# Seven block products instead of eight for gate and up, with a reordered pair pipeline

## Chip, cores and metric

The kernel runs on one core of one Trainium2 chip. The metric is device time in microseconds for one execution. Three executions of the kernel before took 2089.64, 2089.70 and 2092.26 us; the median is 2089.7.

## What is computed

For 32 sequences of 512 tokens with 256 channels, all in float32: a normalized copy of x goes through a delta-rule attention block and an MLP, is added to x, and then a gated MLP is added. Cut to what matters:

```
h = layernorm(normalize(x));  q, k, v = split(h @ gates_w + gates_b);  lr = h @ lr_w + lr_b
k = k / norm(k);  A = tril(k k^T, -1) + I;  u = solve_triangular(A, v)
y = (q k^T) (lr * u);  x1 = normalize(x) + y @ out_w + out_b
x2 = x + x1 + relu(layernorm(x1) @ w1 + b1) @ w2 + b2          # 256 wide
g  = normalize(x2)
out = x2 + (silu(g @ Wg^T) * (g @ Wu^T)) @ Wd^T                # Wg, Wu: 768 x 256, Wd: 256 x 768
```

The weights Wg, Wu and Wd come as integers and are scaled by 1/127. The change is mainly in how the two products of the last line, gate and up, are formed.

## The kernel before, in words

Sequences are worked in 16 pairs (NS = 2). A pair passes through stages, and the stages of three pairs overlap: while gate and up of pair `old` run, the triangular solution of pair `new` is interleaved with them, the pair `following` is loaded and normalized, and the down projection of pair `older` ends. The order of TensorE, VectorE, ScalarE and SP is the order in which the Python code issues instructions (`manual_schedule`); GpSimd's order is left to the framework's scheduler. Work that runs beside the products, a `Side` (L136), is a generator that is advanced in proportion to the columns that TensorE has been given: each product calls `spend(columns)`, and INVERT, PREPARE and INVERT_FIRST say over how many columns a Side is to be spread.

The stages that the prediction uses:

- **Values** (`values_phase`, L1174): gather (pf, L805), through_values (pz), through_keys (pm; its sum m with a bias row is VectorE's, L828), answer (po_d, L844, then statistics L408 to L419), for each sequence of the pair. Before, the keys (pk, L562) and grams (pg, L591) of the following pair stand between these.
- **Inverse** (`invert`, L632): of the following pair's 32x32 diagonal blocks, on VectorE alone. `give` (L601) writes the blocks to DRAM (`given`), SP reads them back spread over partitions (`blocks`), then come a reciprocal (L649), a few sums and fifteen rounds of a product (L683) and a reduction (L689). The result goes through DRAM (`found`, `yb`, `yfull`).
- **Solution** (`solve` and `merge`, L770 and L712): merges the inverted blocks (pw and py, L730 to L763) and solves (pr L784, pu L794), step by step, with VectorE and ScalarE between the steps.
- **Middle** (`middle`, L1055): the residual sum (L903), the MLP (`mlp_in` pa L911, `mlp_out` po_m L844), the normalization for gate and up. `normed` writes h by ScalarE (L422) and transposes 32x32 blocks by VectorE (L460); they go out to DRAM (`way`) and `turned` fetches them back feature-wise (hT).
- **Gate and up** (`gated`, L931): for each of 6 blocks of 128 hidden features and each sequence, two products of 128x512 for gate and two for up (contraction over 256 channels), SiLU by ScalarE from PSUM (L947), product by VectorE from PSUM (L949).
- **Down** (`Down`, L952): already by seven block products instead of eight. `plain` makes three of them (po_x) and then mixes hidden blocks by four GpSimd sums (L987 to L990), `combined` makes the other four (po_y) and adds the parts with VectorE and GpSimd.

A matmul of float32 shows as two records each on PE and PEld. PSUM has three pools: ps_a (3 tiles), ps_f (4 tiles) and one fixed tile.

The inner loop of gate and up reads, with the calls that advance the Sides:

```
for f in range(NF):
    nc.tensor.matmul(pp, lhsT=w[:, f, ts(o, P)], rhs=s.hT[:, f, :],
                     start=(f == 0), stop=(f == NF - 1))
    spend(512)
    if f == NF - 1:
        if name == "gate":
            nc.scalar.activation(natural(g), grouped(pp), AF.Silu)
        else:
            nc.vector.tensor_tensor(natural(g), natural(g), grouped(pp), ALU.mult)
```

Of the kernel before, what the change touches and what calls it, by code (L numbers as in the profile page):

```python
# [22 lines left out]
def kernel(  # L23
# [40 lines left out]
    LEAD = 8  # L64
    NS = 2
    PLAIN = 12
    PREPARE = 12 * 1024
    INVERT = 26 * 1024
# [29 lines left out]
    class Columns:  # L98
# [3 lines left out]
        def __init__(self, n):  # L102
# [4 lines left out]
            first = small.tile([B, self.nc, B], F32, tag="unit", name=f"first{n}", bufs=2)  # L107
# [206 lines left out]
    wgT = const.tile([P, NF, HID], F32, name="wgT")  # L314
    wuT = const.tile([P, NF, HID], F32, name="wuT")
# [6 lines left out]

    class Dequant:
        def __init__(self, src, name, tag, bufs, k):
# [3 lines left out]
            for r0 in range(0, rows // P, k):  # L328
                m = min(k, rows // P - r0)
                wi = wk.tile([P, m, self.cols], I32, tag=tag, name=f"{name}_i{r0}", bufs=bufs)  # L330
                self.parts.append((r0, m, wi))
# [23 lines left out]
    def whole_rows(dst):  # L355
        def put(cc, r0, m, pt):
            nc.scalar.copy(dst[:, cc, r0 * P : (r0 + m) * P], pt)

        return put

    class Combined:


        def __init__(self):
            self.b12 = wk.tile([P, NP, P], F32, tag="p", name="b12")
# [70 lines left out]
    def to_features(src, dst, tag, plain=False):  # L436

        for f in range(NF):
            pt = ps_f.tile([P, 512], F32, tag="mm", name=f"tp_{tag}_{f}")
# [43 lines left out]
    def normalized(s):  # L483
# [15 lines left out]
        yield  # L499

        left = small.tile([P, NT], F32, tag="left", name=f"left_{n}")
        for c in range(NT):
# [4 lines left out]
            yield  # L507
# [9 lines left out]
        for c in range(NT):  # L517
# [4 lines left out]
            nc.gpsimd.tensor_copy(s.hlast[:, c, :], s.a[:, c, C - 1 : C])  # L522
            nc.gpsimd.tensor_copy(s.a[:, c, C - 1 : C], s.r2[:, 1, c : c + 1])
            yield
        if n // NS == 1:
# [14 lines left out]
    def rates(s):  # L540
        n = s.n
        s.lr = small.tile([P, NT], F32, tag="lr", name=f"lr_{n}", bufs=5)
        for c in range(NT):
            junk = wk.tile([P, C], F32, tag="junk", name=f"jl_{n}_{c}", bufs=1)
# [5 lines left out]
        nc.vector.tensor_tensor(s.lr, s.lr, s.r2[:, 0, :], ALU.mult)  # L550
        yield

    def to_keys(s):
        to_features(s.a, s.ag, f"a{s.n}", plain=True)
# [58 lines left out]
    def norms(g, given, seqs):  # L613
# [7 lines left out]
        yield 4  # L621
# [5 lines left out]
        for slot, s in enumerate(seqs):  # L627
            s.kn = kn[:, slot, :]
            nc.vector.tensor_tensor(s.kn, s.kn, s.r2[:, 0, :], ALU.mult)
        yield  # L630

    def invert(g, given, seqs):  # L632
# [20 lines left out]
        )  # L653

# [7 lines left out]
        )  # L662
        nc.vector.tensor_tensor(odd, odd, above, ALU.add)
# [3 lines left out]
        yield 2 * B  # L667
# [12 lines left out]
        for i in range(2, B, 2):  # L680
# [11 lines left out]
            yield 2 * (B + i)  # L692

# [76 lines left out]
    def solve(s):  # L770
# [6 lines left out]
        for i in range(NT):  # L777
# [19 lines left out]
            nc.scalar.mul(s.dp[:, i, :], pu, s.lr[:, i : i + 1])  # L797
            yield

    def contract(s, lhs, rhs, nk, name):  # L800

        s.pp = ps_a.tile([P, NF, C], F32, tag="mm", name=f"p{name}_{s.n}")
# [302 lines left out]
    def first_values(seqs, following, norms_, inverse, given):  # L1105
# [39 lines left out]
        for s in seqs:  # L1145
            fetch_residual(s)
# [214 lines left out]
```

## Time and profile before

| | |
|---|---|
| median of three executions | 2089.7 us |
| the profiled execution | 2090.19 us, span 2088.4 us |
| granted TensorE clock, mean | 0.995 |
| TensorE weight load busy | 1373.5 us (66%) |
| VectorE busy | 1232.8 us (59%) |
| ScalarE busy | 703.9 us (34%) |
| GpSimd busy | 729.9 us (35%) |
| steady pair, start of pf to start of the next pair's pf | 124.2 to 126.3 us |
| first product on TensorE | 21.84 us |

A row of a group names line, engine, operation, the tiles (out<-in) and shapes; after the bar stand busy time, mean nanoseconds of one, and the engine's idle time in front of such instructions with what ended it. A row of the timeline has start, duration (us), engine, line, operation, tiles and count; in brackets stands the idle time before it. A row of windows has the stretch, its length, busy time and instruction count of PE, PEld, VectorE, ScalarE and GpSimd, the granted clock, the DMA share and GB/s.

### The profile page before, as it was taken

To read this page: it belongs to the slowest core of one execution; us is meant where nothing else is said; L and a number is where in the kernel's file an instruction comes from. 1 tells how busy PE (TensorE), PEld (TensorE's weight loads), DVE (VectorE), ACT (ScalarE), POOL (GpSimd) and SP (SyncE) were. 2 spreads that over 40 slices of the span, in tenths; PEclk is the share of its full clock that TensorE was granted. 3 is DMA by queue.
4 is the path that set the end of the run, shared out by engine and by line. 5 is a ranking of instruction groups with operands and counts; after the bars stand their busy time and mean duration, and the time that the engine had idled before them with its cause. 6 is when DMAs were issued, how large, how long until landed. Compare 5 with 4: busy or idle time off the path is not lost.

```text
span 2088.4 us, 27547 instructions
## 1 busy us (share of the span) xinstructions
PE 2028.3 (97%) x9134; PEld 1373.5 (66%) x9134; DVE 1232.8 (59%) x3691; ACT 703.9 (34%) x1788; POOL 729.9 (35%) x1008
## 2 busy tenths in 40 slices
PE   5899999999999999999999999999999999999998
PEld 2565766757576675766767576675766767576675
DVE  3656474755747576474855747476474855747252
ACT  3333423324242343423334242343423334242231
POOL 3411332525224342432525224251422525124244
PEclk9999999999999999999999999999999999999999
DMA  3211332332324223332332324223332432323020
GB/s 90 83 34 28 84 98 62 109 90 56 91 71 127 63 74 89 92 90 62 107 95 54 94 69 128 62 74 89 87 95 62 113 88 54 94 69 107 22 61 21
DMA packets 249605, 163.90 MB, mean 78 GB/s; under 512 B 82129, under 2 KB 225112, under 8 KB 249464
## 3 DMA queue, kind: packets, MB, share of 16 engines
q1 hardware_dynamic: 246272, 160.30, 27.7%
q10 hardware_dynamic: 3112, 1.71, 0.3%
q8 instruction: 73, 1.20, 0.2%
q14 instruction: 68, 0.56, 0.1%
q0 software_dynamic: 80, 0.14, 0.0%
HBM read 96.02 MB, written 66.06 MB: 78 GB/s over the span
## 4 chain that ended last, share of the span: by engine, by line
PE 84%; DVE 7%; DMA 4%; issue 1%; POOL 1%; ACT 1%; SPq 1%; ACTq 0%; POOLq 0%; DVEq 0%
PE pup L940 16%; PE pgate L940 15%; PE pg L591 6%; PE po_d L844 5%; PE pf L805 5%; PE po_y L970 5%; PE pk L562 5%; PE po_x L970 4%; PE pr L784 4%; PE pa L911 4%; PE po_m L844 3%; PE pu L794 3%; PE pm L805 3%; PE pz L805 3%; DMA hT_f<-way_f 1%
## 5 line engine op out<-in xcount | busy, mean ns | idle before, releaser
L940 PE MATMUL pgate<-hT_f,wgT 128*128 128x512 f32 x768 | 366.5, 600 | 8.2 <-DMA hT_f<-way_f 6.3
L940 PE MATMUL pup<-hT_f,wuT 128*128 128x512 f32 x768 | 364.3, 596 | 0.0
L949 DVE TENSOR_TENSOR hid<-hid,pup 128x512 f32<-128x512 f32 x192 | 130.7, 681 | 243.7 <-PE pup L940 240.9
L947 ACT ACTIVATE hid<-pgate 128x512 f32<-128x512 f32 x192 | 113.7, 593 | 404.4 <-PE pgate L940 404.4
L940 PEld LDWEIGHTS pgate<-hT_f,wgT 128*128 128x128 f32 x768 | 142.4, 190 | 153.6 <-issue 135.6
L940 PEld LDWEIGHTS pup<-hT_f,wuT 128*128 128x128 f32 x768 | 143.1, 190 | 146.0 <-issue 139.7
L987 POOL TENSOR_TENSOR hid<-hid 128x384 f32<-128x384 f32 x64 | 63.1, 1007 | 383.0 <-DVE hid L949 383.0
L970 PEld LDWEIGHTS po_y<-wdS,hid 128*128 128x128 f32 x1536 | 176.5, 192 | 8.4 <-issue 6.0
L828 DVE TENSOR_TENSOR m<-pm,obrow 128x256 f32<-128x256 f32 x32 | 13.6, 424 | 280.5 <-ACT m L827 280.4
L970 PE MATMUL po_y<-wdS,hid 128*128 128x128 f32 x1536 | 176.8, 275 | 0.0
L391 POOL TENSOR_TENSOR r_m<-ve_m,neghalf 128x4 f32<-128x4 f32 x32 | 32.4, 1013 | 332.5 <-DVE nmn_m L417 332.4
L591 PE MATMUL pg<-kT 128*128 128x256 f32 (+3 forms) x512 | 144.1, 433 | 0.1
L970 PEld LDWEIGHTS po_x<-wdS,hid 128*128 128x128 f32 x1152 | 132.9, 192 | 8.3 <-issue 4.8
L970 PE MATMUL po_x<-wdS,hid 128*128 128x128 f32 x1152 | 134.1, 275 | 0.0
L591 PEld LDWEIGHTS pg<-kT 128*128 128x128 f32 x512 | 92.0, 190 | 52.9 <-issue 22.4
L562 PE MATMUL pk<-ag,wa 128*128 128x512 f32 x256 | 119.8, 602 | 0.9 <-ACT ag L443 0.9
L911 PE MATMUL pa<-hT_m,w1s 128*128 128x512 f32 x256 | 116.4, 597 | 0.8 <-DMA hT_m<-way_m 0.6
L844 PE MATMUL po_m<-w2s,act 128*128 128x256 f32 x512 | 116.3, 380 | 0.3
L805 PE MATMUL pf<-a,dp 128*128 128x256 f32 x512 | 113.1, 379 | 0.0
L422 ACT ACTIVATE h_f<-a,mr_f,r_f 128x256 f32<-128x256 f32 x112 | 60.6, 594 | 154.0 <-POOL mr_f L419 118.3
L805 PEld LDWEIGHTS pf<-a,dp 128*128 128x128 f32 x512 | 97.3, 190 | 19.6 <-issue 7.2
L689 DVE TENSOR_REDUCE beside<-xt 128x16 f32<-128x64 f32 (+14 forms) x225 | 103.8, 461 | 7.7
(202 smaller groups left out, 3458.0 us busy)
## 6 DMA issues: line engine op xcount, KB each, us to landing
a<-in_L_attn_x_dram SPq DMA_DIRECT2D x32, 512.0 KB, 4.6
x<-in_L_attn_x_dram SPq DMA_DIRECT2D x32, 512.0 KB, 5.5
out_dram<-a SPq DMA_DIRECT2D x64, 256.0 KB, 4.5
way_m<-turn_m SPq DMA_DIRECT2D x120, 128.0 KB, 2.6
hT_m<-way_m SPq DMA_DIRECT2D x30, 512.0 KB, 3.6
way_a<-turn_a SPq DMA_DIRECT2D x112, 128.0 KB, 2.3
ag<-way_a SPq DMA_DIRECT2D x28, 512.0 KB, 3.8
way_f<-turn_f SPq DMA_DIRECT2D x112, 128.0 KB, 2.3
```

Source lines behind the costliest of these rows:

```text
L562: nc.tensor.matmul(pk, lhsT=wa[:, f, ts(o, P)], rhs=s.ag[:, f, :], start=(f == 0), stop=(f == NF - 1),)
L591: nc.tensor.matmul(pg[:, :w], lhsT=s.kT[:, f, ts(j, P)], rhs=s.kT[:, f, j * P :], start=(f == 0), stop=(f == NF - 1),)
L689: nc.vector.tensor_reduce(xc[:, :, i : i + 2], t[:, :, :, :w], axis=AX.X, op=ALU.add)
L784: nc.tensor.matmul(pr, lhsT=s.go[j][:, ts(i - j - 1, P)], rhs=p_[:, j, :], start=(j == 0), stop=(j == i - 1),)
L805: nc.tensor.matmul(s.pp[:, o, :], lhsT=lhs[:, c, ts(o, P)], rhs=rhs[:, c, :], start=(c == 0), stop=(c == nk - 1),)
L844: nc.tensor.matmul(self.po[:, c % 2, :], lhsT=src[:, ts(c, P)], rhs=self.w[:, f, :], start=(f == 0), stop=(f == self.nk - 1),)
L911: nc.tensor.matmul(pa, lhsT=w1s[:, f, ts(o, P)], rhs=s.hT[:, f, :], start=(f == 0), stop=(f == NF - 1),)
L940: nc.tensor.matmul(pp, lhsT=w[:, f, ts(o, P)], rhs=s.hT[:, f, :], start=(f == 0), stop=(f == NF - 1),)
L947: nc.scalar.activation(natural(g), grouped(pp), AF.Silu)
L949: nc.vector.tensor_tensor(natural(g), natural(g), grouped(pp), ALU.mult)
L970: nc.tensor.matmul(po[:, i, :], lhsT=self.A[block][:, j, :], rhs=wdS[:, j, slot, :], start=(j == 0), stop=(j == NP - 1),)
L987: nc.gpsimd.tensor_tensor(A[1, 0], A[1, 0], A[1, 1], ALU.add)
```

## The change

- Gate and up: for two hidden blocks j and the two halves of the channels and of the tokens, seven products of 128x256 take the place of eight. The stationary operands are seven stored blocks (`wgS`, `wuS`, made once by GpSimd sums, `Stationary`); the moving operands are four blocks or sums of blocks of hT (`mixed`, four GpSimd sums a sequence). One PSUM tile `y` gets the products 1, 6, 7 and 4 added one upon another and is copied by ScalarE between them; a second tile `z` gets 2, 5 and, upon 5, 3. Sums and the gate's product are spread over ScalarE, VectorE and GpSimd (`Unit`), with some issued a few steps later (`later`). The steps of a unit are interleaved with those of the unit before.
- Order of a pair: keys, grams and `give` of the following pair move from the values stage into the second half of gate and up (EARLY = 56, every second step). The inverse's Side is begun at the start of the values stage and finished before answer(two). The Down work that stood in the middle moves partly into the values stage. The merge and the first solution step stand between the MLP's products in `middle`; the rest of the solution follows in gate and up, one step in three.
- `normed(two, "m")` and its fetch move into `middle`; `normed` of the second sequence for gate and up is done in steps within gate and up.
- GpSimd's order is now the order of issue, too.
- The residual x is fetched and its bias added separately (`fetch_residual`, `biased`), later and into other buffers. The scaling of dp by lr moves from ScalarE to VectorE; the products of lr and kn with r move from VectorE to GpSimd; the copies of single columns in `normalized` are joined, four in one.
- `contract` and `answer` take PSUM from ps_f. Weight integers are loaded into other buffers; the first pair is reordered accordingly.

The diff, cut to its core:

```diff
-    LEAD = 8
+    LEAD = 16
...
-    PLAIN = 12
-    PREPARE = 12 * 1024
-    INVERT = 26 * 1024
+
+    LOAD, NORM, STORE, TURN, START, MIX, EARLY = 1, 3, 8, 15, 16, 28, 56
+    PREPARE = 13 * 1024
+    INVERT = 17 * 1024
...
+        def put(self, cc, r0, m, pt):
+            dst, some = self.dst, slice(r0 // 2, (r0 + m) // 2)
+            pt = pt.rearrange("p (j i r) -> p j i r", i=2, r=P)
+            nc.scalar.copy(dst[:, some, cc, :], pt[:, :, 0, :])
+            nc.scalar.copy(dst[:, some, 3, :] if cc else self.a21[:, some, :], pt[:, :, 1, :])
+            if cc == NF - 1 and r0 + m == NH:
+                b = lambda i: dst[:, :, i, :]
+                two = lambda o, x, y, op: nc.gpsimd.tensor_tensor(o, x, y, op)
+                two(b(4), self.a21, b(3), ALU.add)
+                two(b(6), b(0), self.a21, ALU.subtract)
+                two(b(5), b(4), b(0), ALU.subtract)
+                two(b(2), b(1), b(5), ALU.subtract)
...
-            nc.scalar.mul(s.dp[:, i, :], pu, s.lr[:, i : i + 1])
+            nc.vector.tensor_scalar(s.dp[:, i, :], pu, s.lr[:, i : i + 1], None, ALU.mult)
...
+        minus(t1, block(0, 1), block(0, 0))
+        yield
+        minus(t2, block(1, 1), t1)
+        yield
+        minus(t3, block(1, 1), block(0, 1))
+        yield
+        minus(t4, block(1, 0), t2)
+        yield
...
+        def copy(self, name, src):
+            t = wk.tile([P, T // 2], F32, tag="x2", name=f"{name}_{self.name}", bufs=4)
+            nc.scalar.copy(t, src)
+            return t
+
+        def p1(self, later):
+            self.y = ps_f.tile([P, 512], F32, tag="mm", name=f"py{self.name}")
+            self.y = self.y[:, : T // 2]
+            self.mul(self.y, 1, True, True)
+            self.top = wk.tile([P, 2, T // 2], F32, tag="fz", name=f"top_{self.name}", bufs=4)
+            nc.scalar.copy(self.top[:, 0], self.y)
+
+        def p2(self, later):
+            self.z = ps_f.tile([P, 2, T // 2], F32, tag="mm", name=f"pz{self.name}")
+            self.mul(self.z[:, 0], 2, True, True)
+
+        def p5(self, later):
+            self.mul(self.z[:, 1], 5, True, True)
+            self.five = self.copy("five", self.z[:, 1])
+
+        def p6(self, later):
+            self.mul(self.y, 6, False, True)
+            nc.scalar.copy(self.top[:, 1], self.y)
+
+        def p7(self, later):
+            self.mul(self.y, 7, False, True)
+            v = self.copy("v", self.y)
+            if self.up:
+                nc.gpsimd.tensor_tensor(v, v, self.five, ALU.add)
+                later(5, lambda: nc.gpsimd.tensor_tensor(
+                    self.out(1, 1), self.out(1, 1), self.half(v), ALU.mult
+                ))
+            else:
+                to = self.out(1, 1)
+                nc.gpsimd.tensor_tensor(to, self.half(v), self.half(self.five), ALU.add)
+                later(10, lambda: nc.scalar.activation(to, to, AF.Silu))
+
+        def p4(self, later):
+            self.mul(self.y, 4, False, True)
+            if self.up:
+                nc.vector.tensor_tensor(
+                    self.out(1, 0), self.out(1, 0), self.half(self.y), ALU.mult
+                )
+            else:
+                nc.scalar.activation(self.out(1, 0), self.half(self.y), AF.Silu)
+
+        def p3(self, later):
+            self.mul(self.z[:, 1], 3, False, True)
...
+            if self.up:
+                nc.vector.tensor_tensor(self.top, self.top, self.z, ALU.add)
+                later(4, lambda: nc.gpsimd.tensor_tensor(
+                    natural(g), natural(g), grouped(flat(self.top)), ALU.mult
+                ))
+            else:
+                nc.vector.tensor_tensor(
+                    natural(g), grouped(flat(self.top)), grouped(flat(self.z)), ALU.add
+                )
+                later(9, lambda: nc.scalar.activation(g, g, AF.Silu))
...
+            steps = [
+                (new, "p1"), (old, "p7"), (old, "p3"), (new, "p6"), (old, "p4"), (new, "p2"),
+                (new, "p5"),
+            ]
...
+        mlp_in(one, 0)
+        normed(two, "m")
+        mlp_in(one, 1)
+        turned(two, "m")
         residual(one)
...
+        if rest:
+            sides_[0].finish()
+        more()
         mlp_out(one, 0)
         mlp_out(one, 1)
+        for d in rest[:2]:
+            d.store()
+        step()
+        more()
+        step()
+        normed(one, "f")
         mlp_in(two, 0)
+        step()
+        residual(two)
         mlp_in(two, 1)
...
+        step()
         mlp_out(two, 0)
...
+        turned(one, "f")
+        if not rest:
+            sides_[1].finish()
+            next(sides_[0].gen)
+            sides_[0].finish()
+        whole(mixed(one))
+        step()
         mlp_out(two, 1)
...
+        sides_ = sides_of(begun(following, given), INVERT)
...
+        some(10)
         whole(gather(one))
-        prep.finish()
+        next(units).both()
+        fetch_residual(one)
+        whole(through_values(one))
         some(2)
+        next(units).both()
+        whole(through_keys(one))
+        third = next(units)
+        third.plain()
+        answer(one)
+        third.mix()
+        biased(one)
         whole(gather(two))
...
+        normed(one, "m")
+        next(combined)()
+        fetch_residual(two)
         whole(through_values(two))
...
+        last = next(units)
+        last.plain()
         whole(through_keys(two))
...
+        turned(one, "m")
         in_order(a)
...
+        biased(two)
+        next(combined)()
+        sides_[1].finish()
+        next(sides_[0].gen)
         answer(two)
+        last.mix()
         in_order(b)
...
+                for i, _ in enumerate(gated(old)):
+                    if i >= EARLY and i % 2 == 0 and solved:
+                        next(early, lambda: None)()
+                    if i % 3 == 2:
+                        solved = next(sol, sol) is sol
```

## The prediction, made before the change was run

> **What bounds the kernel now.** I read the page's busy shares first, then the windows of single pairs, then the order of instructions in time.
>
> ```profile
> PE 2028.3 (97%) x9134; PEld 1373.5 (66%) x9134; DVE 1232.8 (59%) x3691; ACT 703.9 (34%) x1788; POOL 729.9 (35%) x1008
> 463.07:587.31 124.24, 123.96 (x562) 84.13 (x561) 77.65 (x232) 42.75 (x109) 44.52 (x61) 1.00 0.32 86
> L940 PE MATMUL pgate<-hT_f,wgT 128*128 128x512 f32 x768 | 366.5, 600 | 8.2 <-DMA hT_f<-way_f 6.3
> L940 PE MATMUL pup<-hT_f,wuT 128*128 128x512 f32 x768 | 364.3, 596 | 0.0
> ```
>
> TensorE is the bound: 97% of the span, and in a steady pair 123.96 of 124.24 us, at a granted clock of 1.00. A pair leaves VectorE 46 us idle, ScalarE and GpSimd about 80 each. Overlapping records make busy time longer than pace, so I take pace from starts in the timeline:
>
> ```profile
> 741.70 3.62 PE L844 MATMUL po_d<-m,aT 128*128 128x256 f32 x16
> 745.15 4.48 PE L591 MATMUL pg<-kT 128*128 128x512 f32 x16
> 791.33 1.88 PE L940 MATMUL pup<-hT_f,wuT 128*128 128x512 f32 x4
> 793.05 1.88 PE L940 MATMUL pgate<-hT_f,wgT 128*128 128x512 f32 x4
> ```
>
> A float32 matmul is two records ("passes"). Sixteen of 256 columns take 745.15 - 741.70 = 3.45, 0.2155 us each; four of 512 take 1.72, 0.429 each. Passes of 128 columns come out at 0.112. Counted with these (each row's count divided by 16 pairs), a pair needs: gate and up 96 x 0.429 = 41.2, all else 81.6, together 122.8 us. Twelve pairs from 463.07 to 1965.55 average 125.2, so 2.4 us a pair are waits.
>
> **The change, part by part.** *Products.* Two blocks of 128 hidden features were 8 passes of 512 (3.43 us); they become 14 of 256 (3.02). There are 32 x 3 x 2 = 192 such units: 192 x 0.415 = **79.7 us** off TensorE, 5.0 a pair. All passes change weights already in the rows above, so more weight loads cost nothing that the 0.2155 does not hold.
>
> *Sums.* A gate and an up unit (6.03 us of TensorE) now give ScalarE eight copies of 256 (0.37 by the L796 row) and three SiLUs (0.47, 0.47, 0.59): 4.5 us for 1.2 before. VectorE gets 0.68 + 0.68 + 0.42 for 1.36. GpSimd gets three sums of 256 columns and a product of 512. L991 shows 0.74 for 256, L988 1.00 for 384, so 1.33 for 512: 3.55 us. Block sums of the moving side (L975) are 4 x 0.74 = 3.0 a sequence. Six units of each kind and two sequences a pair, with the scaling of dp moved to VectorE (8 x 0.42) and column copies joined: ScalarE 43 to 59, VectorE 78 to 84, GpSimd 44.5 to about 69 us, of a pair of 120. None becomes the bound by its sum. The pieces matter where TensorE waits for them.
>
> The Trainium skill speaks against the move to GpSimd (GPSIMD Engine Reference, "Elementwise — side-by-side cycle accounting": two-input float32 work takes about 2.6 cycles an element there, roughly twice VectorE's time, so VectorE stays the rule). By its figure 256 columns are an estimated 0.56 us, by L991 0.74; the row decides. On VectorE the 27 us of GpSimd would be some 15, but nothing is on TensorE's path while GpSimd keeps within its 6.03 us. The same page's "Specifications" warn that both engines share SBUF interfaces when VectorE reads two SBUF inputs, and here the trace agrees:
>
> ```profile
> 752.75 1.75 DVE L903 TENSOR_TENSOR a<-a,x 128x1024 f32<-128x1024 f32 x1
> 753.37 1.99 POOL L988 TENSOR_TENSOR hid<-hid 128x384 f32<-128x384 f32 x1
> 764.41 1.22 DVE L903 TENSOR_TENSOR a<-a,x 128x1024 f32<-128x1024 f32 x1
> ```
>
> Side by side 1.75 and 1.99; apart 1.22 and 1.00. Most new VectorE work reads PSUM with one input, so I charge only 0.5 us to a residual sum that meets a block sum, off the path.
>
> *The round trip.* One PSUM tile is added to four times, with a ScalarE copy between. A copy starts 0.20 after the next pass would, takes 0.37, and TensorE goes on 0.06 later (m at 117.12 + 0.37, po_d at 117.55): 0.63. Mostly two other products (0.86) lie between: covered, by 0.23. Between p7 and p4 of the last unit there is one: 0.2 a pair.
>
> *Order.* Keys and grams of the next pair go into the second half of gate and up, the inverse from there into the values stage, the merge and first solution steps between the MLP products. What was spread over 26 x 1024 columns (INVERT; at 1.68 ns a column 45 us) gets 17 x 1024, 29 us. Costed by queue, with t = 0 at the first pf:
>
> ```profile
> 749.67 0.27 ACT L595 COPY gd<-pg 128x128 f32<-128x128 f32 x1
> 749.96 1.73 SPq L609 DMA_DIRECT2D given<-gd  x4
> 753.37 0.53 SPq L636 DMA_DIRECT2D blocks<-given  x1
> 758.90 0.36 DVE L649 RECIPROCAL few<-blocks 128x32 f32<-128x32 f32 x1 [4.40 <-DMA blocks<-given]
> 764.01 0.22 DVE L683 TENSOR_TENSOR xt<-beside,blocks 128x64 f32<-128x64 f32 x1
> ```
>
> From issuing the diagonal blocks on SP to the reciprocal: 8.94 us; the inverse's beginning: 5.1. In the new order the last gram ends three products before t = 0, 1.5 with the wait above; so (copy of the gram, 0.2 + 0.27) the blocks go out at -1.0 and VectorE can start at 7.9, after idling. Behind that, in VectorE's one queue, stand before answer(two)'s input: beginning 5.1, fifteen loop rounds 13.2 (summed from the same timeline), two m sums 0.7, answer(one) with statistics 3.5, its transposes 1.5, one combined() 1.3: 25.3, plus 0.7 waiting for po_d. So m(two) is there at 33.9. TensorE would need it after pf 2 x 3.45, pz and pm 4 x 1.72, po_x 4 x 2.02, po_y 2 x 2.7, po_d 3.45 = 30.7. **Wait: 3.2 us a pair**, part at answer(one), part at answer(two).
>
> The middle, followed in the same way: po_d(two) runs from 34.0 to 37.4, VectorE ends its statistics at 39.4, GpSimd's r and mr end at 40.9, ScalarE's four h copies at 43.0. Behind those copies on ScalarE stands the ReLU of mlp_in(one, 1), so po_m starts at 43.9 where TensorE was free at 37.4 + 3.43 + 2.7 = 43.5: 0.4. On VectorE the residual sum, a combined() and both statistics of one end at 49.4, the first merge's three transposes at 50.3, its rhs and the second's transposes at 51.6; TensorE is free at 50.1 and 50.9: pw waits 0.2 and 0.75. The transposes for normed(one, "f") stand behind the merge's copies and end at 55.2; from there to hT_f it takes 7.7 (774.97 to 782.67 before), so 62.9, against 62.3: 0.6. **About 2.0 in all**; the merge's own waits now (PE on xparts, 11.5 us in the run) are replaced, not added. Then r_f(two) stands behind four L975 sums on GpSimd, its h copies stop ScalarE, and behind them wait top_up, v and the next solution step: **0.8**. Bounds for each of these three: nothing if the front work comes 1 us earlier, twice as much if VectorE lags 2 us more; I take what the rows give.
>
> Sum: 3.2 + 2.0 + 0.8 + 0.2 = 6.2 for 2.4 now: 3.8 given back, times 14 pairs = 53 us. The first pair's finish of the inverse leaves over half of 18.3 us to VectorE at once, with 4.7 of TensorE work before a product needs VectorE: +6 (2 to 8). The last unit's sums on GpSimd stand before the last po_x, and own() is queued behind the mixes: +2. -79.7 + 53 + 6 + 2 = -19. The profiled execution took 2090.2 us (span 2088.4), half a microsecond over the median 2089.7: **2071**.
>
> **Rivals.** *The backlog does not reach TensorE.* If the inverse begins 1 us sooner (blocks landed in 4.0 to 6.3 us) and PSUM slots and slack take the rest, the 3.2 fall away: 14 x 3.2 = 45, giving 2026. For it: everything else in that stage has cover. Against: the 25.3 us are queued in order, and 30.7 - 7.9 is only 22.8.
>
> *Slower: foreign ScalarE work breaks the round trip.* Place: gate and up. Twelve operations a pair with no TensorE work of their own (four h of 0.59, eight centering passes of 0.50) enter ScalarE's queue between the copies; the cover to spare is 0.23. If each falls before a copy that is due, it costs 0.5 - 0.23 = 0.27: 3.2 a pair, 49 over 15, less the 11 that I already charge for h: 2109. With a wait for nm or mr in front, twice that. It decides from 19 / 15 = 1.3 us a pair, 0.11 an operation. For it: h_f waited 118.3 us in all for mr_f before. Against: most centering passes now follow p7, where the next copy is two products off.
>
> *No saving at all*, because shorter passes do not run in half the time: excluded by 0.2155 against 0.429.
>
> **How the numbers follow.** Main case, most of the saving given back, 2050 to 2094: 0.45, of it 0.07 within 0.2% (about what a measurement of this kernel can tell from no change, 4 us) and the rest faster. Backlog absorbed, 2010 to 2050: 0.2. Slower, 2094 to 2150: 0.35. So faster 0.58, same 0.07, slower 0.35. Leaving out 0.08 below and 0.12 above, the range is 2030 to 2118.
>
> **What would show it.** Gate and up products of 256 columns at 0.2155, 2688 of them; TensorE waits on VectorE's m before po_d near 3 us a pair, with VectorE without idle from the reciprocal to the end of the inverse; pw on xparts about 1; the reciprocal some 8 us after pf. Wrong would be: no idle time at po_d (first rival), or idle time in front of p6, p4, p3 on ScalarE's copies throughout gate and up (second).

## The result, and the profile after

Four executions took 2150.16 to 2152.22 us, median 2150.5, against 2090.05 for the kernel before beside it (four, 2089.64 to 2092.26): ratio 1.0287, 95% interval 1.0273 to 1.0301. The change is slower by 60 us; the forecast was 2071. The profiled execution has a span of 2148.7 us at a mean granted clock of 0.987.

From the page of the kernel after: busy shares, the chain of work that ended last by engine, and three groups.

```profile
PE 1998.5 (93%) x10286; PEld 1590.2 (74%) x10286; DVE 1372.7 (64%) x3851; ACT 924.0 (43%) x2532; POOL 1112.0 (52%) x1400
...
PE 50%; DVE 24%; DMA 8%; issue 7%; ACT 6%; POOL 3%; SPq 1%; ACTq 0%; DVEq 0%; POOLq 0%
...
L1043 POOL TENSOR_TENSOR v_up<-v_up,five_up 128x256 f32<-128x256 f32 x96 | 69.8, 727 | 241.4 <-ACT v_up L1017 241.4
...
L1003 PE MATMUL pygate<-hS,wgS 128*128 128x256 f32 x576 | 174.8, 385 | 5.2 <-ACT v_gate L1017 2.4
...
L1067 POOL TENSOR_TENSOR hid<-hid,top_up 128x512 f32<-128x512 f32 x96 | 122.4, 1275 | 0.0
```

The same chain in the kernel before:

```profile
PE 84%; DVE 7%; DMA 4%; issue 1%; POOL 1%; ACT 1%; SPq 1%; ACTq 0%; POOLq 0%; DVEq 0%
```

TensorE was the path for 84% of the span and is now for 50%; VectorE's share went from 7% to 24%. Counted from the starts of all passes, each at its own pace (0.2155 us for 256 columns and so on), TensorE's work fell from 1967.8 to 1887.9 us: 79.9 saved, as forecast. What lies beyond that pace between two starts is waiting. It rose by 140 us.

Where, the windows tell. First a steady pair of the kernel after (start of pf to the next), then another cut into its stages: values (to the first po_d of the second sequence that waits), middle (to the first product of gate and up), gate and up. Columns: stretch, length, busy time and count of PE, PEld, VectorE, ScalarE, GpSimd, clock, DMA share, GB/s.

```profile
503.20:632.40 129.20, 121.93 (x633) 96.95 (x632) 86.20 (x243) 56.34 (x157) 67.36 (x86) 1.00 0.30 82
632.47:665.30 32.83, 31.48 (x204) 28.73 (x202) 28.45 (x87) 9.36 (x23) 22.48 (x26) 1.00 0.29 82
665.30:696.04 30.74, 28.07 (x174) 21.06 (x175) 24.94 (x73) 9.52 (x23) 16.06 (x23) 1.00 0.40 112
696.04:760.69 64.65, 62.59 (x256) 47.19 (x257) 33.72 (x85) 37.49 (x112) 28.89 (x38) 1.00 0.24 69
```

A pair of the kernel before in nearly the same cuts:

```profile
714.00:745.15 31.15, 31.15 (x126) 23.34 (x125) 9.39 (x35) 10.83 (x24) 8.15 (x8) 1.00 0.18 55
745.15:782.67 37.52, 37.20 (x233) 30.67 (x232) 30.15 (x96) 14.68 (x37) 24.61 (x29) 1.00 0.40 101
782.67:839.00 56.33, 56.05 (x205) 30.45 (x206) 37.50 (x104) 17.34 (x48) 11.01 (x24) 1.00 0.33 92
```

(Before, the cut between values and middle lies at the end of that po_d, because there it does not wait.) VectorE is busy 28.45 + 24.94 = 53.4 of the 63.6 us of values and middle, 84%; before it was 39.5 of 68.7, 58%. Over the whole pair it is busy only 67%, and by such a sum the forecast held that no engine becomes the bound. Keys and grams, 15.5 us of TensorE work (6.9 + 8.6), have left exactly these two stages. The middle by itself lost the second gram (4.3) and 120 Down passes of 128 columns (13.4), which now stand in the values stage.

Waits of a steady pair, mean of 13 pairs, by stage in us (the last column is from the first experiment):

| | before | after | after, but eight products |
|---|---|---|---|
| values | 0.25 | 2.25 | 2.73 |
| middle | 0.64 | 4.01 | 4.02 |
| hT_f, first product of gate and up | 0.65 | 1.20 | 1.19 |
| inside gate and up | 2.04 | 4.43 | 0.48 |
| sum | 3.58 | 11.89 | 8.42 |

The table of TensorE's waits for the kernel after names the releasers (total us, times, longest):

```profile
PE pw L756 <- DVE xparts L749: 21.8, 31, 4.2
PE po_d L870 <- DVE m L854: 20.7, 17, 1.3
PE pygate L1003 <- DMA hT_f<-way_f: 15.0, 14, 2.6
PE pygate L1003 <- DVE hid L1071: 11.5, 13, 0.9
PE pzgate L1003 <- POOL hS L975: 8.6, 1, 8.6
PE po_m L870 <- ACT act L951: 8.5, 1, 8.5
PE pk L586 <- DMA ag<-way_a: 5.5, 11, 0.9
```

Five rows come in most of the pairs; the waits of 8.5 and 8.6 us come once, in the first pair. By windows: 13 steady pairs add 8.3 each (108 us), the first pair 20 (31.7 us of waits for 11.5), the rest 12. (The first pair became 30.6 us longer and the fifteenth 15.2 shorter, because one pair's keys and grams moved from one window to the other.)

### The profile page after: what moved, and what is told of

It reads as the page before. It is cut to its first block, busy times and chain, and to the rows that moved or that the text cites. A ratio compares the mean times of both kernels' runs of the same rounds, so it can differ in the third digit from the quotient of the medians.

```text
span 2148.7 us, 31430 instructions
## 1 busy us (share of the span) xinstructions
PE 1998.5 (93%) x10286; PEld 1590.2 (74%) x10286; DVE 1372.7 (64%) x3851; ACT 924.0 (43%) x2532; POOL 1112.0 (52%) x1400
## 4 chain that ended last, share of the span: by engine, by line
PE 50%; DVE 24%; DMA 8%; issue 7%; ACT 6%; POOL 3%; SPq 1%; ACTq 0%; DVEq 0%; POOLq 0%
PE pg L615 6%; PE pyup L1003 6%; PE pygate L1003 6%; PE pk L586 5%; PE pzup L1003 4%; PE pzgate L1003 4%; PE po_x L1125 4%; PE pr L810 3%; DVE xt L708 3%; PE po_d L870 3%; DMA hT_f<-way_f 3%; DVE beside L714 3%; PE pf L831 2%; PE pu L820 2%; DMA ag<-way_a 2%
## 5 line engine op out<-in xcount | busy, mean ns | idle before, releaser
L1043 POOL TENSOR_TENSOR v_up<-v_up,five_up 128x256 f32<-128x256 f32 x96 | 69.8, 727 | 241.4 <-ACT v_up L1017 241.4
L1003 PE MATMUL pygate<-hS,wgS 128*128 128x256 f32 x576 | 174.8, 385 | 5.2 <-ACT v_gate L1017 2.4
L1003 PE MATMUL pyup<-hS,wuS 128*128 128x256 f32 x576 | 175.8, 387 | 1.5 <-ACT v_up L1017 0.4
L1071 DVE TENSOR_TENSOR hid<-top_gate,pzgate 128x512 f32<-128x512 f32 x96 | 65.2, 679 | 144.0 <-PE pzgate L1003 144.0
L1049 POOL TENSOR_TENSOR hid<-v_gate,five_gate 128x256 f32<-128x256 f32 x96 | 69.7, 726 | 151.3 <-ACT v_gate L1017 151.3
L1003 PEld LDWEIGHTS pygate<-hS,wgS 128*128 128x128 f32 x576 | 107.6, 191 | 42.4 <-issue 21.0
L1003 PEld LDWEIGHTS pyup<-hS,wuS 128*128 128x128 f32 x576 | 105.0, 190 | 44.0 <-issue 13.4
L870 PE MATMUL po_d<-m,aT 128*128 128x256 f32 x448 | 105.6, 383 | 18.9 <-DVE m L854 18.9
L1067 POOL TENSOR_TENSOR hid<-hid,top_up 128x512 f32<-128x512 f32 x96 | 122.4, 1275 | 0.0
L1003 PE MATMUL pzup<-hT_f,wuS 128*128 128x256 f32 x384 | 116.0, 384 | 3.9 <-ACT five_up L1017 3.8
L1003 PE MATMUL pzgate<-hT_f,wgS 128*128 128x256 f32 x384 | 117.2, 387 | 0.0
```

The lines of the kernel that those rows point to most:

```text
L870: nc.tensor.matmul(self.po[:, c % 2, :], lhsT=src[:, ts(c, P)], rhs=self.w[:, f, :], start=(f == 0), stop=(f == self.nk - 1),)
L1003: nc.tensor.matmul(dst, lhsT=self.w[:, self.j, self.SLOT[i], :], rhs=self.s.B[i], start=first, stop=last, skip_group_check=True,)
L1043: nc.gpsimd.tensor_tensor(v, v, self.five, ALU.add)
L1049: nc.gpsimd.tensor_tensor(to, self.half(v), self.half(self.five), ALU.add)
L1067: later(4, lambda: nc.gpsimd.tensor_tensor(natural(g), natural(g), grouped(flat(self.top)), ALU.mult))
L1071: nc.vector.tensor_tensor(natural(g), grouped(flat(self.top)), grouped(flat(self.z)), ALU.add)
```

## The experiments

All are the kernel after with one edit unless said; times are medians, to be held against 2150.5.

**Is it the order or the products?** e1_eight: gate and up by eight products of 128x512 in the new order, without `mixed` and the sums.

```diff
-            steps = [
-                (new, "p1"), (old, "p7"), (old, "p3"), (new, "p6"), (old, "p4"), (new, "p2"),
-                (new, "p5"),
-            ]
+                    for f in range(NF):
+                        nc.tensor.matmul(
+                            pp, lhsT=w[:, j, 2 * i + f, :], rhs=s.hT[:, f, :],
+                            start=(f == 0), stop=(f == NF - 1),
+                        )
```

> The new order with the eight products of 128x512 and the sums of the kernel before (SiLU and product straight from PSUM, no block sums of hT). Gate and up then cost TensorE 5.0 us a pair more than in the changed kernel. Order theory: of 11.9 us of waits in a steady pair some 7 (po_d on m, pw and py in the middle, hT_f, pk on ag) are the new order's and stay; only the 3.4 at the products' own PSUM tiles go. 16 x (5.0 - 3.4) = +26: about 2176. Rival, the products' additional work on ScalarE, VectorE and GpSimd makes everything late: waits fall to the 3.6 of the kernel before, 16 x 5.0 - 14 x 8.3 = -36: about 2114.

2175.2 us (ratio to the kernel before 1.0399, 1.0382 to 1.0416). That is the order theory's number to the microsecond. The last column of the table above shows why: values, middle and hT_f wait as long with eight products; only the waits inside gate and up are the seven products' own (3.95 us). So the order costs 4.8 us a pair, the products' pieces 3.5, and the products save 5.0. Neither alone explains the loss: 5.0 - 3.5 would still be a gain.

**Does the chain on one PSUM tile make TensorE wait?** e2_unchained:

```diff
-            self.mul(self.y, 6, False, True)
+            self.mul(self.other, 6, True, True)
-            self.mul(self.y, 7, False, True)
+            self.mul(self.y, 7, True, True)
-            self.mul(self.y, 4, False, True)
+            self.mul(self.other, 4, True, True)
```

> Products 6, 7 and 4 no longer add to the tile that ScalarE has just copied: each starts anew, 1 and 7 in one half of the PSUM tile, 6 and 4 in the other, so gate and up are not the reference's; every instruction is still there. TensorE waits for a copy only two products back. Chain theory: the waits in front of pygate and pyup inside gate and up (2.3 us a pair) go: 15 x 2.3 = -35, about 2115. Rival, the waits come from queues of foreign work that hold PSUM tiles: they show up as waits for a new tile instead, 2140 to 2150.

2150.6 us, and 4.61 us of waits in gate and up as against 4.43. But the edit took away the addition and not the wait. In this run's trace, too, no product 7 starts less than 0.14 us and no product 4 less than 0.05 us after the end of the copy that it waited for before, although the products 4 and 7 now write different halves of the tile. 27 of 180 products 4 start within 0.12 us of that end, as many as in the kernel after. So this run does not say what the chain costs. TensorE's waits in it are those of the kernel after, v_gate among them (2.7 us here, 2.4 there):

```profile
PE pygate L1003 <- DVE hid L1071: 11.6, 13, 0.9
...
PE pygate L1003 <- ACT v_gate L1017: 2.7, 15, 0.6
```

What the products wait for can be counted in the trace of the kernel after, product by product (mean of 13 pairs; a wait also delays the second pass of its product, by some 0.1 us, which is included):

- 2.0 us a pair stand behind copies of ScalarE. Of these 0.7 are where a single product of another unit lies between: from 6 to 7 in the first unit of a pair (0.36) and from 7 to 4 in the last (0.37). In 1.3 ScalarE does something else just ahead of the copy: 0.4 are `h_f` of the second sequence, 0.9 the centering passes (L525) of the next pair, 0.5 of them at one product 3:

```profile
730.50 0.50 ACT L525 ACTIVATE a<-a,nm 128x256 f32<-128x256 f32 x1
730.99 0.36 ACT L1017 COPY five_up<-pzup 128x256 f32<-128x256 f32 x1
731.40 0.70 PE L1003 MATMUL pzup<-hT_f,wuS 128*128 128x256 f32 x2 [0.27 <-ACT five_up L1017]
```

- 1.15 is the first product of the second sequence behind VectorE's hid (1.05 without the second pass), 0.65 is the keys on ag; the rest is small.

The largest single wait is that on hid. VectorE's sum L1071 is late there because four normalizing passes (L541, 2.80 us) stand ahead of it. Two edits went at this.

e7_spaced: `yield 3` instead of `yield` behind each of those passes, the Side's weight 2 * 50 for 2 * 42.

> The four normalizing passes of 0.70 us that VectorE does for a sequence of the following pair are issued at a third of the rate (each weighs 3 in the side's generator instead of 1). Theory: at the start of the second sequence's gate and up the product waits 1.05 us a pair for a PSUM tile that VectorE's sum (hid from pzgate) reads, and that sum stands behind these four passes; spaced they leave it through: -0.9 to -1.1 a pair over 13, 2136 to 2139. Rival: VectorE is then late with ag, and the keys wait for it: 2148 to 2155.

2167.6 us: the wait on hid fell from 11.5 to 6.1 us, but pygate's wait on v_gate rose from 2.4 to 16.6. On ScalarE the copy v_gate of the second sequence's first unit now stands behind a centering pass that waits for VectorE's nm, and product 4 waits 1.2 us a pair for that copy:

```profile
734.57 0.51 ACT L525 ACTIVATE a<-a,nm 128x256 f32<-128x256 f32 x1 [0.96 <-DVE nm L520]
...
735.07 0.35 ACT L1017 COPY v_gate<-pygate 128x256 f32<-128x256 f32 x1
```

e15_banks: `self.z` is taken ahead of `self.y` in p1.

> A unit takes its two PSUM tiles in the other order (z before y, both at product 1), nothing else. Theory: the tile for y comes from the bank that was free first, and that is the z of the unit before the last, whose reader is VectorE's sum; with the order swapped y follows y, read by ScalarE, and the 1.05 us a pair at the start of the second sequence go: -0.9 to -1.1 over 13 pairs, 2136 to 2139. Rival: z is then needed sooner or y's own reader is late: 2148 to 2156.

2152.0 us, the wait on hid 11.6: not the order of the two tiles. That VectorE's foreign work makes hid late is supported by the first of these two; which dependence of the product waits for L1071 stays open.

**Is the merge what waits in the middle?** e3_merge_late:

```diff
-        step = lambda: rest and next(sol, None)
+        step = lambda: None
```

> The merge and the first solution step leave the middle; all steps of the solution follow in gate and up, one in three. Nothing else is moved. Theory: VectorE is late in the middle, so pw and py wait there (2.7 us a pair) and hT_f comes late (1.2); in gate and up these steps have cover. -3 to -3.9 a pair over 14: 2096 to 2108. Rival: in gate and up the merge's transposes queue behind the products' sums and hold up TensorE as much: 2140 to 2155.

2157.9 us. The theory fell. The waits on xparts went, and others stood in their place:

```profile
PE pa L945 <- DMA hT_m<-way_m: 26.7, 13, 2.8
PE pygate L1003 <- DMA hT_f<-way_f: 23.5, 13, 2.7
```

The merge had been filling time in which TensorE would wait for hT_m of the second sequence anyway. The chain that ended last, kernel after, from the late sum m to hT_f (start, length, what) shows the path; none of its pieces between the first and the last line is TensorE's:

```profile
665.30 1.58 PE po_d L870 x6
666.90 0.88 DVE a L876 x2
...
672.49 1.58 ACT h_m L444 x3
674.09 0.45 DVE turn_m L482
...
680.90 0.20 DVE xparts L748
...
683.55 0.21 DVE uv L1166
683.78 0.42 DVE uv L1166
684.20 0.34 DVE a L1166
...
684.89 0.29 DVE wparts L759
685.20 0.47 ACT wparts L762 x2
685.69 2.08 ACT h_f L444 x4
687.80 0.45 DVE turn_f L482
...
689.64 2.30 DMA way_f<-turn_f
691.96 0.03 SPq L495
...
692.02 3.98 DMA hT_f<-way_f
```

**Is that a latency with TensorE free beside it?** e14_cover puts unread work there; e16_one_step needed work.

```diff
         more()
+        for d in rest[2:3]:
+            spare = ps_f.tile([P, 4, P], F32, tag="mm", ...)
+            d.products(spare, [(0, (0, 0), 3), (2, (1, 0), 5), (3, (0, 1), 6), (1, (1, 1), 4)])
         step()
```

> Adds to the middle of 14 pairs, behind the second combined() and ahead of the merge's first products, once more the 24 passes of 128 columns of that combined(), into a PSUM tile that nobody reads: 2.7 us a pair of TensorE work and nothing on any other engine. Theory: TensorE waits in the middle for a chain over VectorE, ScalarE and two transfers that does not depend on it; the added products fill those waits (pw 1.6, pa and py 0.9) and leave the end of the middle where it was: 0 to +0.7 a pair, 2150 to 2160. Rival: the waits are set relative to TensorE's own products and stay behind the added ones: +2.7 a pair, 2185 to 2190.

2146.1 us: 14 x 2.7 = 38 us of additional products, and the run is not longer. Waits in the middle fell from 4.01 to 1.59; of the 21.8 us of pw this is left:

```profile
PE pygate L1003 <- DMA hT_f<-way_f: 10.7, 14, 1.8
...
PE pw L756 <- DVE xparts L749: 5.6, 3, 4.2
```

e16_one_step adds one `step()` behind `mlp_out(two, 1)`.

> One more step of the solution (two products of 256 columns, four passes of 0.2155) stands in the middle, behind the last mlp_out and ahead of gate and up, where TensorE waits 1.2 us for hT_f. Theory: they run in that wait, and are gone from gate and up: -0.5 to -0.9 a pair over 13, 2139 to 2144. Rival: their input, VectorE's copy, comes behind the statistics, so they wait themselves and push gate and up back: 2150 to 2158.

2134.4 us, -16: more than expected. The wait on hT_f fell from 15.0 to 3.0 us. Little came in its place: pr on dp 1.6 us in the run, one pg on kT 1.9, and 1.0 more at the first pair's pzgate. Waits inside gate and up fell by 0.4 a pair.

**The wait of po_d in the values stage.** e11_half_inverse:

```diff
         for i in range(2, B, 2):
+            if g and i >= 16:
+                yield 2 * (B + i)
+                continue
```

> Leaves out rounds 16 to 30 of the inverse (eight of fifteen) for all pairs but the first, so the inverse is unfinished and the output is not the reference's; that takes about 8.9 us a pair off VectorE ahead of the second sequence's sum m, and nothing else. Theory: VectorE's backlog there sets the end of the values stage and with it the middle; the waits of po_d (1.9), of pw, py and pa in the middle (some 3) and of hT_f (1.2) go: -4 to -6 a pair over 14, 2066 to 2094. Rival: only po_d's wait is the backlog's, the middle waits for its own statistics and transfers and gives back the rest: -1.9 a pair, 2122 to 2128.

2119.5 us: near the rival's number, 2.5 us below its range. Waits in values fell from 2.25 to 0.59, in the middle they stayed (4.17): the middle's chain starts at po_d(two), so it moves with it, and each stage pays for itself. That is 22 us over 13 pairs; another 7 went from the first pair's window, where the shorter inverse of the next pair is finished. Could the inverse start sooner instead?

e9_early_give: `(i % 2 == 0 or i >= 70)` for `i % 2 == 0` in front of the next keys and grams.

> From step 70 of gate and up the next keys and grams follow at every step instead of every second, so the diagonal blocks of the following pair's second sequence go out about seven products (2.8 us) earlier; nothing else moves. Theory: from the reciprocal to hT_f the path runs along VectorE without a gap, and it starts 2.7 us late, when blocks land; what the start gains, the whole stage gains: -1.9 to -2.7 a pair over 14, 2113 to 2124. Rival: the chain is set behind that start (the DMA of hT_m and hT_f, the merge), or keys now wait for ag: no more than -0.5 a pair, 2143 to 2152.

2148.3 us, no more than the rival allowed. The reciprocal came 3.7 us after pf instead of 6.0, but the second po_d ended only 0.2 sooner. The head start is spent at the first sequence: between the reciprocal and the second sum m VectorE is idle for 4.0 us instead of 2.0, 1.6 of them (0.6 in the kernel after) for po_d(one) and 1.1 (none) for ScalarE's part of the first sum m. First a pair of this run (pf at 628.6), then one of the kernel after (pf at 632.5):

```profile
633.15 0.36 DVE L672 RECIPROCAL few<-blocks 128x32 f32<-128x32 f32 x1 [0.95 <-DMA blocks<-given]
640.15 0.42 DVE L854 TENSOR_TENSOR m<-pm,obrow 128x256 f32<-128x256 f32 x1 [0.24 <-ACT m L853]
643.56 0.88 DVE L876 SCALAR_TENSOR_TENSOR a<-po_d,r,a 128x256 f32<-128x256 f32 x2 [1.61 <-PE po_d L870]
...
638.73 0.36 DVE L672 RECIPROCAL few<-blocks 128x32 f32<-128x32 f32 x1 [2.68 <-DMA blocks<-given]
645.49 0.41 DVE L854 TENSOR_TENSOR m<-pm,obrow 128x256 f32<-128x256 f32 x1
647.63 0.88 DVE L876 SCALAR_TENSOR_TENSOR a<-po_d,r,a 128x256 f32<-128x256 f32 x2 [0.35 <-PE po_d L870]
```

The rounds that could go on stand behind sums that read TensorE's results. Rounds that come sooner wait at these places. e13_early_inverse also packs the rounds (LEAD = 8, INVERT = 13 * 1024).

> Blocks go out early as before (every step from step 70), and the inverse's rounds are issued closer together and sooner (LEAD 8, 13 x 1024 columns), so that none of them stands directly ahead of the second sequence's sum m on VectorE. Theory: po_d waited because the last rounds stood there in VectorE's order, not because VectorE lacked time: the wait goes as it did with half the inverse left out (2119), less what the earlier rounds cost at answer(one): 2118 to 2130. Rival: rounds that come sooner hold up answer(one) by as much: 2143 to 2152.

2164.1 us: in the run po_d's wait on m fell from 20.7 to 9.8 us, but po_m on act rose from 8.5 to 16.9, pw from 21.8 to 26.8, pa on hT_m from 1.9 to 7.0. That is worse than the rival. e6_late_inverse goes the other way (inverse over 26 * 1024 to step 18 of gate and up, merge and solution from step 30, hS of the first sequence in other buffers):

> In every pair the inverse is spread over 26 x 1024 columns from the start of the values stage and finished at step 18 of gate and up; merge and solution follow from step 30; keys and grams of the next pair stay early, from where the solution ends. Theory: with the inverse no longer ahead of answer(two) on VectorE, the wait of po_d on m (1.8 us a pair) goes, and the second sequence's hT_m, which was late by 2.25 us in the run with the late merge, comes in time: against that run -4 to -5 a pair over 14 and some 15 in the first pair, 2080 to 2100. Rival: that stage is bound by the chain from answer to hT_m and hT_f itself, because the keys and grams that covered it are gone; the waits on hT_m and hT_f stay: 2130 to 2155.

2293.1 us. po_d waits no more; hT_f waits 48.5 us in the run, pw 51.9, po_m on act 36.2. The stretch from po_d(two) to hT_f became 32.8 us (30.7 from the late sum m in the kernel after) though the merge has left it, and the waits inside gate and up more than doubled, from 4.4 to 9.8 us a pair. So the longer inverse makes the middle's chain longer still. In gate and up it meets merge and solution, and what each costs there was not separated.

**Relief for VectorE.** e10_residual_pool: `nc.gpsimd` for `nc.vector` in `residual`.

> The two residual sums of a pair (1.22 us each on VectorE, in the middle) are GpSimd's. Theory: VectorE's queue is the path through the middle, so taking 2.4 us off it brings hT_f forward by 1.2 to 2.4 us a pair: 2116 to 2134. Rival: GpSimd needs some 2.7 us for each and stands behind other sums, VectorE's next sum upon the same tile waits for it, and nothing or less than nothing is left: 2150 to 2170.

2165.9 us. hT_f's wait fell to 5.2 us, pw's rose from 21.8 to 35.7: VectorE's next sum on the same tile (L883) waits 30.1 us in the run for GpSimd.

**The order of before with the seven products.** e8_old_order (also hS of the first sequence in buffers that the inverse does not hold):

> The seven products and their sums in the order of the kernel before: keys and grams back in the values stage between its products, the inverse from the middle to step 28 of gate and up, merge and solution from step 36, Down in the middle; GpSimd still in order of issue. The new order then costs nothing, and of the changed kernel's waits only the products' own remain. By the run with eight products the order costs 8.4 - 3.6 = 4.8 us a pair, the products' own waits 11.9 - 8.4 = 3.5: a pair is 121.6 - 5.0 + 3.6 + 3.5 = 123.7, 1.5 below the kernel before; with the first pair near its old time 2060 to 2075. Rival: the two do not add; in the old order the solution's ScalarE and VectorE steps fall between the products' copies and cost what the order did: 2110 or more.

2262.2 us; the additive theory fell. e12_old_order_2 gives GpSimd's order back to the scheduler and puts `mixed(one)` ahead of two Down sums:

> The seven products in the order of the kernel before once more, with two things changed against the first such run: GpSimd's order is the scheduler's again, as in the kernel before, and the block sums of the first sequence stand ahead of the Down sums of the middle. Theory: what that run lost (20.3 us of waits a pair, 4.2 of them on the block sums, 3.9 on a sum of po_m, 2.9 on hT_f) was GpSimd's order, and is gone: 2060 to 2090. Rival: in that order the middle ends with statistics, hT_f, block sums and the inverse on the same two engines, whoever orders GpSimd: 2200 or more.

2197.2 us, 132.2 a pair, with this at the top:

```profile
PE pzgate L1008 <- POOL hS L980: 43.0, 14, 3.6
```

The block sums come late because of GpSimd's order, not for want of its time. In every steady pair they stand behind a Down sum for which GpSimd waits 2.6 us:

```profile
960.38 0.99 POOL L1177 TENSOR_TENSOR a<-a,uv 128x384 f32<-128x384 f32 x1 [2.62 <-DVE a L1171]
961.33 1.41 POOL L980 TENSOR_TENSOR hS<-hT_f 128x256 f32<-128x256 f32 x2
```

So the parts do not add in this form. A version with the block sums ahead of all Down sums was not tried, and whether the seven products gain anything in the old order stays open.

**The first pair.** e4_first_act issues `normed(one, "f")` behind `mlp_in(two, 1)` there.

> Only in the first pair, the normalization of its first sequence for gate and up is issued behind mlp_in of the second, so that ScalarE's ReLU no longer stands behind a wait for GpSimd's mr_f. The wait of 8.6 us of po_m on act goes. VectorE, which idled 5.0 us for that po_m with the inverse queued behind it, ends the inverse 5 us sooner, so the second wait (8.6 us, pzgate on hS) does not grow by all of it: -5 us, and up to -6 more if the clock is not halved after the wait: 2139 to 2146. Rival: the inverse alone decides when hS can be written, the second wait grows by what the first loses: 2149 to 2151.

2147.6 us. One of the two waits went and the other became 6.2, with 4.5 new at the transposes behind turn_f. e5_first_pair adds hS in other buffers and the inverse spread to step 18 of gate and up (solution from step 30):

> Only the first pair is changed: the block sums of its first sequence get buffers that the running inverse does not hold; the inverse is spread over the middle and the first 18 steps of gate and up in place of being finished in one go before gate and up; the solution starts at step 30; normalization for gate and up is issued behind mlp_in of the second sequence. Theory: of the first pair's 32 us of waits both long ones (8.6 and 8.6 us) go and with them the halved clock that follows idle time (some 12 us of lost pace): -20 to -29, 2122 to 2130. Rival: the work on VectorE is the same, so the wait comes back as products waiting for VectorE's sums, and the later solution delays keys and grams: -8 or less, 2142 to 2150.

2140.9 us: the first pair's waits fell from 31.7 to 25.2 us and its clock from 0.92 rose to 0.94. That is half of what was expected or less; VectorE's inverse is still there.

**Together.** e17_sum is e5, e16 and e9; e18_sum_down also moves one combined() from the values stage to the middle.

> The three edits that helped, together: the first pair's own buffers, later inverse and later normalization (-9.5 alone), one solution step in the wait for hT_f (-16 alone), keys and grams at every step from step 70 (-2 alone). If they are independent, 2150.5 - 9.5 - 16 - 2 = 2123: 2118 to 2128. Rival, the waits replace one another (first pair and steady pairs do not share a wait, but the early grams and the solution step both move what gate and up holds): 2130 to 2140.

> As the sum of the three, and the second combined() of the values stage (2.7 us of TensorE, 1.3 us of VectorE) goes into the middle, ahead of the merge's first products, its store with it. Theory: the middle has 2.7 us free a pair, as the unread products showed; the values stage loses 2.7 us of cover ahead of answer(two), and VectorE 1.3 us of work in front of the sum m, so po_d waits 1.4 longer at most: -1.3 a pair over 13 against the sum, about 2106, 2098 to 2116. Rival: po_d waits for the whole 2.7 us, and VectorE's four additional sums delay the middle: 2122 to 2145.

2124.8 us (1.0157, 1.0131 to 1.0183) and 2194.1. The three add up as forecast, as far as e9's 2 us can be told from noise. The move cleared the wait for xparts in the middle as e14 had, but po_d's wait rose from 1.8 to 6.7 us a pair: the values stage has no TensorE work to give. And py waits 1.7 instead of 0.4 for the copies wparts. No version here beats the kernel before.

## Why the prediction was wrong

Right were: the saving (79.7; 79.9 counted); the engines' sums (ScalarE 59, VectorE 84, GpSimd 69 forecast; 56.3, 86.2, 67.4 in the pair from 503.20); GpSimd's row instead of the figure of the Trainium skill (GPSIMD Engine Reference, "Elementwise — side-by-side cycle accounting"; 0.74 against an estimated 0.56 for 256 columns: 0.73 here; 1.33 for 512: 1.28).

The forecast gave back 61 us in all: waits of 6.2 us a pair for 2.4, over 14 pairs, and 8 for first pair and tail. Measured: 140. The steps that failed (the first two weigh about the same):

- **"About 2.0 in all" for the middle: 5.2** (4.01 and hT_f 1.20). The chain from the late sum m to hT_f has a length of its own, 30.7 us, and TensorE has work for 25.5 of them; the forecast gave the chain 28.9 (34.0 to 62.9) and TensorE 28.3, waits included. The missing 1.8 lies between the merge's first transposes (the last ends 17.7 us after the chain's start, forecast 17.6) and the end of the transposes for hT_f (22.9, forecast 21.2). There a second combined() has its sums (L1166 in the chain above, 1.4 us) ahead of the copies wparts, for which h_f waits; the forecast counted one combined(). po_m (0.40) came as forecast, pw at the merge's start is 1.6 for 0.95, and the later merge steps (pw 0.8 at L776, py 0.4) and pa (0.55) were taken as covered. e14 shows that it is a latency: 2.7 us more work, same time. The forecast noticed that keys and grams left and counted it as a move at no cost; they and the moved Down passes were the cover.
- **The 0.8 behind r_f(two) and the round trip's 0.2: 4.43.** The forecast's own two places are there: copies behind h_f of the second sequence (0.4 for 0.8) and from 7 to 4 in the last unit (0.37 for 0.2). Put at nothing were the same place from 6 to 7 in the first unit (0.36), VectorE's normalizing passes ahead of the sum hid (1.15), the keys on their transfer ag (0.65), and the centering passes on ScalarE ahead of copies (0.9), which only the slower rival charged.
- **"First pair +6": +20.** The finish of the inverse on VectorE was foreseen. Not foreseen were that hS of the first sequence has the buffer (tag "blocks") that the running inverse holds, so that GpSimd waits for its end, and that on ScalarE a ReLU stands behind normalizations that wait for GpSimd. e5, which removes both and spreads the inverse, gains 9.5 us.
- **po_d 3.2: 2.25.** The mechanism was right (e11), the size 1.4 times too large: the reciprocal came 6.0 us after pf in the mean, not 7.9. The fetch of the blocks went out about when forecast (2.2 us after pf; forecast 2.4), but from there to the reciprocal it took 3.8 us (3.6 to 4.0 in 13 pairs) and not the 5.5 of the row that the forecast used. The queue behind it was right: 26.8 us to the end of the sum m(two), forecast 26.0. In the pair from 632.47 the fetch is this row, the reciprocal follows at 638.73:

```profile
635.01 0.53 SPq L659 DMA_DIRECT2D blocks<-given  x1
```

- The waits before were 3.6 a pair, not 2.4. This worked for the forecast.

In sum: 13 x (8.3 - 3.8) = 58.5, first pair 20 - 6 = 14, rest 12 - 5.8 = 6: 79, against 2150.5 - 2071 = 79.5. The slower rival had the sign, and 2150 at the end of its range, in the main by luck. Its mechanism, foreign work of ScalarE ahead of the copies, is in the trace, but with 0.9 us a pair beside the 0.4 of h_f, where it forecast 3.2; the rest of the loss has other causes. e2 tests it no more than it tests the chain. "No saving" and "the backlog does not reach TensorE" fell with the counts above.

## What to carry to other kernels

Cost a reordering by stage, not by the pair: write down, for the stretch between two points where TensorE must have an operand, the length of the chain on the other engines and TensorE's own work in it; work that is moved out was cover, and costs what the chain then sticks out. An engine at 67% of the period can be at 84% of the stretch that counts. To find out whether a wait is latency, add unread work to it: if the time stays, there is room for needed work. It pays only if the work can be spared where it stood: one solution step in the wait for hT_f gained 16 us (e16), Down work at the place of e14 lost 69 against e17 (e18). And when an edit is to remove a wait, look in its trace whether the wait is gone (e2) before reading the time.

## What the hardware showed

- VectorE kept to its order of issue: work that was ready 2.3 us sooner (e9) gained 0.2 us, because it stood behind operations that read what TensorE and ScalarE had not yet written (idle 1.6 us at po_d(one) in place of 0.6).
- In two long waits the granted clock was halved, and it stayed so for a while after them. In the first pair of the kernel after, the waits of 8.5 and 8.6 us end at 156.1 and 172.9 us; the clock was 0.5 from 151.5 to 161.7 and from 168.5 to 182.2. These 10.2 and 13.7 us are 3 and 4 times 3.41; the Trainium skill ("TensorE: Matmul & The Clock Gate", Part 1) has a free-running window of that length. Behind the waits lie 5.6 and 9.3 us at half speed, at most 7.5 us of lost pace. In the steady pairs, with waits of up to 2.6 us, the clock stayed at 1.00 but for two stretches of 3.4 us (from 953.6 and 1469.0). The window of that pair, with 0.92 as its mean clock:

```profile
103.70:245.80 142.10, 121.83 (x529) 91.70 (x528) 73.86 (x210) 61.02 (x167) 42.32 (x55) 0.92 0.14 38
```
